# Two folded 512x512 weight matrices by quarter blocks, seven block products each, with quarter sums on Pool

## The chip, the cores and the metric

The kernel runs on one core of a Trainium2 chip. The metric is the device time of one execution in microseconds. The core has five engines with instruction streams of their own: PE (matmuls into PSUM), DVE (vector operations), ACT (scalar engine: activations and copies), POOL (GpSimd) and SP (which issues DMAs). [...]

## What is computed

Four layers follow each other on x of shape 8 x 512 x 32 x 32, in float32. The change touches layer 1, an attention with a residual, and stands in time beside layer 0. Cut to what matters:

```python
# layer 0: f, g, h are 1x1 convolutions to 64 channels; f and g get a batch norm and relu
z = einsum('bcn,bcm->bnm', f, g)
sigma = svd(z)[:, 0]                       # the largest singular value of each image
x = conv1x1(einsum('bnm,bcm->bcn', z / sigma, h), Wv) + x
# layer 1
h = group_norm(x)
q, k, v = wq @ h + bq, wk @ h + bk, wv @ h + bv
attn = softmax(einsum('bcn,bcm->bnm', q, k) * scale)
x = x + wp @ einsum('bnm,bcm->bcn', attn, v) + bp
# layers 2 and 3 follow
```

Since q'k is h'(wq'wk)h up to terms in the biases, and wp and wv stand next to each other, the kernel forms two 512x512 matrices once, on the chip: `wu` from q and k, `wo` from v and p. They are used for all eight images.

## The kernel before

The weights come with the contraction on the partitions. 512 channels are four chunks of 128 partitions, so a 512x512 matrix is a tile of 128 x 4 x 512. The program has three parts.

First, layer 0 streams through the eight images (L1225) while the weights are loaded. In the last image `natural` (L1191) turns q, k and v with PE transposes, evicted by ACT and DVE into `nat_q`, `nat_k`, `nat_v`. The batch-norm statistics of layer 0 then go through a serial piece: two small matmuls with `fold`, `rsqrt_eps` (L226 to L231: a power on Pool, L227, and small DVE operations), the relus on ACT (L1340), transposes of f and g (L1117), and gram matrices (L1312).

Second, `chain` squares a 128x128 matrix again and again to get sigma: two matmuls (L1008, L1009), an eviction on DVE and ACT, every second time also a trace (L1036, L1037, L1042) and a reciprocal and its powers (L1069 to L1072). Each step waits for the one ahead of it. To keep PE busy, a generator `filler` yields pieces of other work between the steps: the product that forms `wu`, further grams, the folded biases (L1290). The order of PE is written out by hand here: two filler pieces after one step, one after the next, and so on. After the chain, `entering` lets the first image into layer 1 (L403 to L436: residual, statistics, again a power on Pool), with the rest of the filler, at its end the product that forms `wo`. The orders of DVE, ACT and Pool are found by the scheduler.

A product is 16 matmuls of 128x128 by 128x512 in `product` (L1265), four for each 128 rows of the result, into `wide`, a PSUM tile of two banks, of which there are two. A `wide` is evicted whole by DVE or ACT (L1276, L1278).

Third, the main loop: for each image attention of layer 1, then layers 2 and 3. It begins with the first image: `normal` (eight L453 on DVE), `split_h` (four differences of quarters, L319 to L322), `make_u` (L380 with `wu`). The large products of the main loop already use the method that the change brings to the folding. `sums_of` and `differences_of` form sums and differences of quarters, and `seven` runs seven block products with their evictions: ACT copies at L331 and L342, DVE additions from PSUM at L337, and one addition on Pool at L352. `sums_u` (L1390) forms the sums of the quarters of the finished `wu`, four operations on DVE.

The functions that the diff touches, and what calls them:

Of the kernel before, what the change touches and what calls it, by code (L numbers as in the profile page):

```python
# [8 lines left out]
F32 = mybir.dt.float32  # L9
# [3 lines left out]
ALU = mybir.AluOpType  # L13
# [70 lines left out]
def kernel(  # L84
# [30 lines left out]
    def wide():  # L115
        return psum["wide"].tile([P, N], F32, tag="wide", name="wide")
# [4 lines left out]
    def bank():  # L121
        return psum["bank"].tile([P, HF], F32, tag="bank", name="bank")
# [17 lines left out]
    def half(i):  # L140
        return bass.ts(i, HF)
# [156 lines left out]

        return [t[:, rows[k], cols[m]] for m in range(2) for k in range(2)]

    def sums_of(a, more, queued=False):

        a11, a12, a21, a22 = a
        s1, s2, s4 = more
        tt = nc.vector.tensor_tensor
        first = tt(s1, a21, a22, ALU.add)
        if queued:
            tc.keep_in_program_order(first)
        tt(s2, s1, a11, ALU.subtract)  # L309
        tt(a21, a11, a21, ALU.subtract)  # L310
        tt(s4, a12, s2, ALU.subtract)
        return {"A11": a11, "A12": a12, "A22": a22, "S1": s1, "S2": s2, "S3": a21, "S4": s4}

    def differences_of(b, more):

        b11, b12, b21, b22 = b
        t1, t2, t4, t3 = (list(more) + [b12])[:4]
        tt = nc.vector.tensor_tensor
        tt(t1, b12, b11, ALU.subtract)  # L319
        tt(t2, b22, t1, ALU.subtract)  # L320
        tt(t3, b22, b12, ALU.subtract)
        tt(t4, b21, t2, ALU.subtract)  # L322
        return {"B11": b11, "B21": b21, "B22": b22, "T1": t1, "T2": t2, "T3": t3, "T4": t4}

    def seven(term, c11, c12, c21, c22, b1=None, b2=None, exp=None, then=None):
# [40 lines left out]
            then()  # L366
        yield

    def product_of(lt, rhs, view=None, parts=1):

        def term(ps, ka, kb, first, last):
            fresh = ps is None
            if fresh:
                ps = bank()
            w = HF // parts
            for q in range(parts):
                for k in range(2):
                    mm(  # L380
                        out=ps[:, q * w : (q + 1) * w],
                        lhsT=lt(ka, kb, q, k),
                        rhs=rhs(ka, kb, q, k),
                        start=first and q == 0 and k == 0,
                        stop=last and k == 1,
                        skip_group_check=True,
                    )
            return ps, ps if view is None else view(ps)

        return term  # L390
# [63 lines left out]
        return ht  # L454

    chunks = [slice(0, 2), slice(2, 4)]

    def split_h(env, ht):
        hs = env["big"].tile([P, 3, 2, HF], F32, tag="hs", name="hs")
# [725 lines left out]
    def natural(name, tag):  # L1185
        t = nat[name] = a1.tile([P, CC, C], F32, tag=tag, name="nat_" + name)
        for i in range(CC // 2):
            tp = wide().rearrange("p (o c j) -> p o c j", o=2, j=P)
            for k in range(2):
                for cc in range(CC):  # L1190
                    nc.tensor.transpose(  # L1191
                        tp[:, k, cc, :], sbw[name][:, cc, bass.ts(2 * i + k, P)], ident
                    )
            dst = t[:, 2 * i : 2 * i + 2, :].rearrange("p o (c j) -> p o c j", j=P)
            nc.scalar.copy(dst[:, 0], tp[:, 0])
            nc.vector.tensor_copy(dst[:, 1], tp[:, 1])
            yield
# [15 lines left out]
    for b in range(B):  # L1213
        xt = load_x(b) if b else first
        for name, src, pool in later.get(b, ()):
            load_w(name, src, shapes.get(name, [P, CC, C]), pool)
        if b == 4:
            load_rows()
        if b >= B - 2:
            resident[b] = xt  # L1220
        banks = [bank() for _ in w0]

        def products(i, cc):
            for h in range(NH):
                mm(  # L1225
                    out=banks[i][side(h), :],
                    lhsT=w0[i][:, cc, :],
                    rhs=xt[:, cc, half(h)],
                    start=cc == 0,
                    stop=cc == CC - 1,  # L1230
                )

        if b == 0:
            for cc in range(CC):
                for i in range(2):
                    products(i, cc)
        for i in range(3):
            if b == B - 1 and i == 2:
                for _ in natural("q", "w3"):
                    pass  # L1240
            if b or i == 2:
                for cc in range(CC):
                    products(i, cc)
            if i == 0:
                nc.scalar.copy(fs[b], banks[i])
                nc.vector.bn_stats(st[:, 0, b, :], fs[b])
            elif i == 1:
                nc.vector.tensor_copy(gs[b], banks[i])
                nc.vector.bn_stats(st[:, 1, b, :], gs[b])
                if last is not None:  # L1250
                    turn(last[0], last[1], ht_pair[last[0] // 2], 0)
        hraw = a2.tile([P, HF], F32, tag="hraw", name="hraw")
        nc.scalar.activation(hraw, banks[2], AF.Identity, bias=bhc)
        last = b, hraw
        if b == 3:
            total3 = sign_weights()
        if b == 5:
            scale_signs(total3)

    def product(lt, rhs, dst, vector):  # L1260
        for i in range(CC // 2):
            ps = wide()
            for k in range(2):
                for oc in range(CC):
                    mm(  # L1265
                        out=ps[:, half(k)],
                        lhsT=lt[:, oc, bass.ts(2 * i + k, P)],
                        rhs=rhs[:, oc, :],
                        start=oc == 0,
                        stop=oc == CC - 1,  # L1270
                    )
                    if k == 0 or oc < CC - 1:
                        yield
            to = dst[:, 2 * i : 2 * i + 2, :].rearrange("p o c -> p (o c)")
            if i % 2 and vector:
                nc.vector.tensor_copy(to, ps)  # L1276
            else:
                nc.scalar.copy(to, ps)  # L1278
            yield

    def biases():

# [23 lines left out]

    def gram(j, i, lt, rhs):
        ps = wide()  # L1310
        for t in range(NT):
            mm(  # L1312
                out=ps[:, 0:P],
                lhsT=lt[:, t, :],
                rhs=rhs[:, t, :],
                start=t == 0,
                stop=t == NT - 1,
            )
            if t == NT // 2 - 1:
                yield  # L1320
        nc.vector.tensor_tensor(gm[j][:, i, :], ps[:, 0:P], mask2, ALU.mult)
        yield
# [54 lines left out]
    def sums_u():  # L1377

        a11, a12, a21, a22 = quarters_of(wu, chunks, cols2)
        s1, s2, s4 = (su[:, i] for i in range(3))  # L1380
        weights["u"] = {
            "A11": a11, "A12": a12, "A22": a22, "S1": s1, "S2": s2, "S3": a21, "S4": s4
        }
        for args in (
            (s1, a21, a22, ALU.add),
            (s2, s1, a11, ALU.subtract),
            (a21, a11, a21, ALU.subtract),
            (s4, a12, s2, ALU.subtract),
        ):
            nc.vector.tensor_tensor(*args)  # L1390
            yield

    cols2 = [slice(0, C // 2), slice(C // 2, C)]

    def filler():

        yield from natural("v", "k")
        load_w("p", w_p, [P, CC, C], a1, tag="v")  # L1400
        yield from product(nat["q"], nat["k"], wu, True)
        yield from gram(jl, 2, ht_pair[jl], gtl)
        scale_z()
        yield
        between = biases()
        sums = sums_u()
        for j in rest:
            for _ in grams(j):
                next(sums, None)
                yield  # L1410
                if next(between, "end") != "end":
                    yield
        yield from product(nat["v"], sbw["p"], wo, False)

    todo = filler()
    for _ in range(5):
# [1 line left out]
    for ftl, gtl in turned_pair(jl):  # L1418
        pass
    for i, t in ((0, ftl), (1, gtl)):  # L1420
        for _ in gram(jl, i, t, t):
            pass

    relus = iter([(2 * j + k, i) for j in rest for i in range(2) for k in range(2)])
    with tc.manual_schedule(engines={mybir.EngineType.PE}):
        steps = entering(0)
        for k, _ in enumerate(chain(jl, True)):
            for _ in range(2 - k % 2 if k <= 2 * NSTEP else 4):
                next(todo, None)
            for args in (next(relus, None),):  # L1430
                if args:
                    relu(*args)
        for k in range(CC + 2):
            next(steps)
            for _ in range(3 if k < CC else 5):
                next(todo, None)
        for _ in todo:
            pass
# [193 lines left out]
```

## Time and profile before

The median of three runs is 1932.47 us (1932.23 to 1932.93). The profiled execution took 1932.7, its span is 1930.8 us, and the granted PE clock is 0.998.

| engine | busy us | instructions |
|---|---|---|
| PE | 1906.6 | 6230 |
| DVE | 1158.2 | 1875 |
| ACT | 507.7 | 807 |
| POOL | 229.7 | 178 |

| stretch (us from the start) | PE busy | DVE busy | POOL busy | what runs |
|---|---|---|---|---|
| 100 to 114 | 12.53 | 6.61 | 0.70 | statistics of layer 0, relus, first grams |
| 114 to 162 | 45.98 | 28.60 | 0.55 | squaring chain, with filler |
| 162 to 200.5 | 36.54 | 26.65 | 1.02 | first image into layer 1, product for `wo`, start of `make_u` |

A line of a timeline reads: start in us, duration in us, engine, line of the kernel, operation, output<-input, sizes, count; in brackets the idle time of the engine before it and what ended it. Neighbours of one kind are merged, with their number after x. A float32 matmul is two instructions for PE. In the view of busy time by stretch the columns are the stretch and its length, then busy time and instructions of PE, of the weight loads, DVE, ACT and POOL, the PE clock, the DMA share and GB/s.

### The profile page before, as it was taken

Reading aid. Unit: us, or ns where it says so; the run is one execution under the profiler, and the core shown is the slowest. Engines: PE = TensorE matmul, PEld = TensorE weight load, DVE = VectorE, ACT = ScalarE, POOL = GpSimd, SP = SyncE. Lnnn points to the kernel's source line nnn. Section 1 sums busy time; section 2 is a strip of 40 time slices with the busy share of each in tenths; the row PEclk is TensorE's granted clock in tenths of the full one; section 3 lists DMA queues with packets and bytes.
Section 4 is the critical chain, followed back from the end, with each engine's and each line's share of the span. In section 5 each row is a group of like instructions: output and inputs, shape, how many; then the busy total and the mean of one; then the engine's idle time right before and its main releaser. Section 6 shows DMA issues by size and latency. Waiting matters only on the chain.

```text
span 1930.8 us, 16673 instructions
## 1 busy us (share of the span) xinstructions
PE 1906.6 (99%) x6230; PEld 987.4 (51%) x6230; DVE 1158.2 (60%) x1875; ACT 507.7 (26%) x807; POOL 229.7 (12%) x178
## 2 busy tenths in 40 slices
PE   9999999999999999999999999999999999999997
PEld 4367456544655447454555446544645455544653
DVE  3256677448764687537754676348663775466647
ACT  2141222135222332025212331034202421143114
POOL 0000001200111001300121011201120011201121
PEclk9999999999999999999999999999999999999999
DMA  8420000002000120002000120002000200010001
GB/s 319 154 77 7 1 6 12 1 11 87 17 1 0 33 71 12 1 11 87 17 1 1 33 71 11 1 11 87 11 0 1 84 15 11 0 33 22 11 1 46
DMA packets 27784, 66.47 MB, mean 34 GB/s; under 512 B 4272, under 2 KB 5424, under 8 KB 27056
## 3 DMA queue, kind: packets, MB, share of 16 engines
q1 hardware_dynamic: 26768, 64.90, 10.0%
q8 instruction: 51, 0.84, 0.2%
q10 hardware_dynamic: 864, 0.43, 0.1%
q14 instruction: 37, 0.30, 0.1%
q0 software_dynamic: 64, 0.00, 0.0%
HBM read 38.51 MB, written 18.87 MB: 30 GB/s over the span
## 4 chain that ended last, share of the span: by engine, by line
PE 91%; DVE 7%; ACT 1%; issue 1%; DMA 0%; POOL 0%; DVEq 0%; ACTq 0%
PE bank L380 41%; PE bank L547 20%; PE bank L937 6%; PE bank L796 6%; PE bank L1225 4%; PE bank L648 3%; PE bank L403 2%; PE bank L665 2%; PE bank L1008 1%; PE wide L1265 1%; DVE both L739 1%; DVE both L709 1%; PE bank L1009 1%; PE wide L1312 1%; PE bank L688 1%; PE bank L817 1%
## 5 line engine op out<-in xcount | busy, mean ns | idle before, releaser
L547 PE MATMUL bank<-e,vt 128*128 128x512 f32 x768 | 334.0, 593 | 0.0
L547 PEld LDWEIGHTS bank<-e,vt 128*128 128x128 f32 x768 | 145.0, 190 | 175.4 <-issue 173.2
L380 PE MATMUL bank<-ut,h 128*128 128x512 f32 x384 | 181.3, 596 | 0.0
L337 DVE TENSOR_TENSOR e<-bank,e 128x512 f32<-128x512 f32 x128 | 87.6, 684 | 61.1 <-PE bank L380 60.3
L380 PE MATMUL bank<-us,hs 128*128 128x512 f32 x256 | 122.1, 599 | 1.3 <-DVE us L309 0.5
L380 PEld LDWEIGHTS bank<-ut,h 128*128 128x128 f32 x384 | 71.5, 190 | 85.8 <-issue 83.6
L937 PE MATMUL bank<-e,tpg 128*128 128x512 f32 x256 | 114.7, 595 | 0.0
L796 PE MATMUL bank<-tpg 128*128 128x512 f32 x256 | 114.6, 592 | 0.0
L803 ACT ACTIVATE e<-bank 128x512 f32<-128x512 f32 x128 | 76.5, 597 | 128.5 <-PE bank L796 128.5
L352 POOL TENSOR_TENSOR e<-e 128x512 f32<-128x512 f32 x32 | 44.1, 1378 | 419.5 <-ACT e L331 419.5
L380 PE MATMUL bank<-wo,h 128*128 128x256 f32 x384 | 91.8, 382 | 0.0
L808 DVE TENSOR_TENSOR esum<-esum,e 128x1024 f32<-128x1024 f32 x48 | 58.8, 1226 | 54.5 <-ACT e L803 54.5
L380 PE MATMUL bank<-h,wu 128*128 128x512 f32 x192 | 90.3, 593 | 0.7 <-ACT ut L342 0.7
L337 DVE TENSOR_TENSOR vt<-bank,vt 128x512 f32<-128x512 f32 x64 | 44.0, 688 | 70.5 <-PE bank L380 70.0
L937 PEld LDWEIGHTS bank<-e,tpg 128*128 128x128 f32 x256 | 48.1, 190 | 63.2 <-issue 63.1
L796 PEld LDWEIGHTS bank<-tpg 128*128 128x128 f32 x256 | 48.6, 190 | 60.8 <-issue 60.5
L352 POOL TENSOR_TENSOR ut<-ut 128x512 f32<-128x512 f32 x16 | 21.7, 1359 | 478.2 <-ACT ut L333 478.2
L380 PEld LDWEIGHTS bank<-wo,h 128*128 128x128 f32 x384 | 71.6, 190 | 13.5 <-ACT vt L331 4.1
L380 PEld LDWEIGHTS bank<-us,hs 128*128 128x128 f32 x256 | 46.7, 190 | 56.0 <-issue 46.4
L676 ACT ACTIVATE sg<-xt,rb 128x512 f16<-128x512 f32 x64 | 45.0, 718 | 103.7 <-DVE xt L667 100.2
L825 DVE RECIPROCAL rsum<-bank 128x512 f32<-128x512 f32 x15 | 50.3, 3356 | 28.6 <-PE bank L817 28.6
L1225 PE MATMUL bank<-xt,fg 128*64 128x512 f32 x256 | 59.7, 614 | 4.5 <-DMA fg<-in_w_fg 4.5
(325 smaller groups left out, 3090.1 us busy)
## 6 DMA issues: line engine op xcount, KB each, us to landing
xt<-in_x SPq DMA_DIRECT2D x55, 512.0 KB
out<-both SPq DMA_DIRECT2D x63, 256.0 KB
rfull<-rsum SPq DMA_DIRECT2D x60, 128.0 KB
f_dram<-f SPq DMA_DIRECT2D x8, 256.0 KB
fb<-f_dram SPq DMA_DIRECT2D x8, 256.0 KB
w<-in_w SPq DMA_DIRECT2D x1, 1024.0 KB
q<-in_w_q SPq DMA_DIRECT2D x1, 1024.0 KB
k<-in_w_k SPq DMA_DIRECT2D x1, 1024.0 KB
```

The source lines that it names most:

```text
L337: nc.vector.tensor_tensor(dst, ps, u, ALU.add)
L352: nc.gpsimd.tensor_tensor(c22, c22, c12, ALU.add)
L380: mm(out=ps[:, q * w : (q + 1) * w], lhsT=lt(ka, kb, q, k), rhs=rhs(ka, kb, q, k), start=first and q == 0 and k == 0, stop=last and k == 1 ...
L547: mm(out=ps, lhsT=a[:, t, bass.ts(r_, P)], rhs=e[t], start=first and t == 0, stop=last and t == NTH - 1, skip_group_check=True,)
L648: mm(out=ps[:, i, :], lhsT=xt[:, cc, bass.ts(4 * h + i, P)], rhs=sbw["tpg"][:, cc, 2 * P : 3 * P], start=cc == 0, stop=cc == CC - 1,)
L676: nc.scalar.activation(sg[:, cc, :], xt[:, cc, half(h)], AF.Sign, bias=rb3[:, cc : cc + 1])
L796: mm(out=ps, lhsT=pt[:, 0, bass.ts(t, P)], rhs=tt[:, 0, half(h)], start=True, stop=True,)
L803: nc.scalar.activation(e[:, half(h)], ps, AF.Exp, scale=float(P) ** -0.5)
L808: nc.vector.tensor_tensor(esum, esum, e, ALU.add)
L825: nc.vector.reciprocal(r, ps)
L937: mm(out=banks[h], lhsT=gt[:, t, :], rhs=es[t][:, half(h)], start=t == 0, stop=t == NT - 1,)
L1225: mm(out=banks[i][side(h), :], lhsT=w0[i][:, cc, :], rhs=xt[:, cc, half(h)], start=cc == 0, stop=cc == CC - 1,)
```

## The change

The two products are formed by 2x2 blocks of 256x256. Instead of eight block products there are seven (the form of Strassen and Winograd, as in the main loop), with four sums of the quarters of one factor (S1 to S4), four differences of the other (T1 to T4), and seven additions per block row in the evictions. Of the sums, those of q, v and p, and T3 and T4 of k, go to Pool; T1 and T2 of k to DVE. A term's result is 128x256 in half of a `wide`. The first two grams take `bank` instead of `wide` for their PSUM, and the number of filler pieces taken at the end changes. It is for less matmul work on PE: 7 block products of 8.

```diff
-    def sums_of(a, more, queued=False):
+    def sums_of(a, more, queued=False, eng=nc.vector):
...
-        tt = nc.vector.tensor_tensor
+        tt = eng.tensor_tensor
...
-    def differences_of(b, more):
+    def differences_of(b, more, engs=(nc.vector,) * 4):
...
+        for eng, (to, first, second) in zip(
+            engs, ((t1, b12, b11), (t2, b22, t1), (t3, b22, b12), (t4, b21, t2))
+        ):
+            op = eng.tensor_tensor(to, first, second, ALU.subtract)
+            if eng is nc.gpsimd:
+                tc.keep_in_program_order(op)
...
-    def product_of(lt, rhs, view=None, parts=1):
+    def product_of(lt, rhs, view=None, parts=1, source=bank, width=HF):
...
+                sums_q = sums_of(
+                    quarters_of(nat["q"], chunks, cols2),
+                    [so[:, i] for i in range(3)],
+                    eng=nc.gpsimd,
+                )
...
-    def product(lt, rhs, dst, vector):
-        for i in range(CC // 2):
-            ps = wide()
-            for k in range(2):
-                for oc in range(CC):
-                    mm(
...
-            if i % 2 and vector:
-                nc.vector.tensor_copy(to, ps)
-            else:
-                nc.scalar.copy(to, ps)
-            yield
+    def differ(rhs, to, engs):
+        b = [rhs[:, chunks[k], cols2[n]] for k in range(2) for n in range(2)]
+        return differences_of(b, to, engs)
+
+    def product(ab, dst):
...
+        for i in range(2):
+            term = product_of(
+                lambda ka, kb, q, k: a[ka][:, k, bass.ts(i, P)],
+                lambda ka, kb, q, k: b[kb][:, k, :],
+                source=lambda: next(source),
+                width=C // 2,
+            )
+            lo, hi = dst[:, i, :], dst[:, 2 + i, :]
+            yield from seven(term, lo[:, cols2[0]], lo[:, cols2[1]], hi[:, cols2[0]], hi[:, cols2[1]])
...
-    def gram(j, i, lt, rhs):
-        ps = wide()
+    def gram(j, i, lt, rhs, source=wide):
+        ps = source()
...
+        t3 = a1.tile([P, 2, C // 2], F32, tag="absw", name="t3")
+        engs = (nc.vector, nc.vector, nc.gpsimd, nc.gpsimd)
+        qk = sums_q, differ(nat["k"], [su[:, i] for i in range(3)] + [t3], engs)
...
-        yield from product(nat["q"], nat["k"], wu, True)
+        yield from product(qk, wu)
...
+                elif vp is None:
+                    vp = (
+                        sums_of(
+                            quarters_of(nat["v"], chunks, cols2),
+                            [so[:, i] for i in range(3)],
+                            eng=nc.gpsimd,
+                        ),
+                        differ(sbw["p"], [free[:, i] for i in range(3)], (nc.gpsimd,) * 4),
+                    )
-        yield from product(nat["v"], sbw["p"], wo, False)
+        yield from product(vp, wo)
...
-        for _ in gram(jl, i, t, t):
+        for _ in gram(jl, i, t, t, bank):
...
-            for _ in range(3 if k < CC else 5):
+            for _ in range(3 if k <= CC else 6):
```

## The prediction

> **What bounds it now.** I read the page first, then busy time by stage, then the timelines of the stretch that the change touches (100 to 200 us). The first two lines are from the page, the next three from the view of busy time by stretch.
>
> ```profile
> span 1930.8 us, 16673 instructions
> ...
> PE 1906.6 (99%) x6230; PEld 987.4 (51%) x6230; DVE 1158.2 (60%) x1875; ACT 507.7 (26%) x807; POOL 229.7 (12%) x178
> ...
> 100.00:114.00 14.00, 12.53 (x79) 8.88 (x77) 6.61 (x23) 10.06 (x16) 0.70 (x1) 1.00 0.54 189
> 114.00:162.00 48.00, 45.98 (x320) 38.00 (x321) 28.60 (x119) 15.26 (x35) 0.55 (x1) 1.00 0.06 23
> 162.00:200.50 38.50, 36.54 (x168) 21.35 (x168) 26.65 (x63) 6.31 (x10) 1.02 (x1) 1.00 0.03 8
> ```
>
> PE is busy nearly all the time, so less matmul work is worth its full length, unless PE then waits for something else. Between 100 and 200 us it idles only 5.5 of 100 us, and Pool does almost nothing (three instructions). But in this stretch PE is full because the products L1265 are filler between the steps of serial chains: statistics of layer 0, then the squaring chain (L1008, L1009, L1042), then the statistics of layer 1. Two timelines show these chains.
>
> ```profile
> 103.07 0.70 POOL L227 TENSOR_TENSOR r_r<-r_v,minus_half 128x2 f32<-128x2 f32 x1 [91.68 <-DVE r_v L226]
> 103.80 0.16 DVE L228 TENSOR_TENSOR r_e<-r_r 128x2 f32<-128x2 f32 x1 [0.20 <-POOL r_r L227]
> ...
> 105.70 1.52 ACT L1340 ACTIVATE f<-f,bi,r_r 128x512 f32<-128x512 f32 x2 [1.57 <-DVE bi L1370]
> ...
> 114.09 0.49 PE L1008 MATMUL bank<-gm 128*128 128x128 f32 x2 [0.38 <-DVE gm L1321]
> ```
>
> A tiny power on Pool releases six tiny DVE operations, these the relus, these the transposes and grams, these the squaring chain. Whatever delays DVE at 104 us delays 114.09.
>
> ```profile
> 189.20 7.11 PE L1265 MATMUL wide<-p,nat_v 128*128 128x512 f32 x16
> ...
> 192.18 3.74 DVE L453 TENSOR_SCALAR h<-xt,r_r,bi 128x512 f32<-128x512 f32 x8
> 195.83 1.22 DVE L319 TENSOR_TENSOR hs<-h 128x1024 f32<-128x1024 f32 x1
> ...
> 200.52 1.88 PE L380 MATMUL bank<-hs,su 128*128 128x512 f32 x4
> ```
>
> DVE normalises the first image while PE still runs the second product. By the chain of waits PE leaves that product at 196.31 and goes on into L380 with no wait for h.
>
> [...]
>
> ```profile
> 702.28 0.16 DVE L1070 TENSOR_TENSOR r<-r 128x1 f32<-128x1 f32 x1
> ...
> 710.28 1.26 POOL L352 TENSOR_TENSOR e<-e 128x512 f32<-128x512 f32 x1 [14.83 <-ACT e L331]
> ...
> 710.57 0.99 DVE L1070 TENSOR_TENSOR r<-r 128x1 f32<-128x1 f32 x1
> ```
>
> The same 128x1 product takes 0.16 us alone and ends with the Pool instruction otherwise (710.28 + 1.26 against 710.57 + 0.99). [...]
>
> **The change, part by part.**
>
> *Matmuls.* Before: 16 of 128x512 per product; a f32 matmul is two instructions in the trace, and the chain of waits gives 6.97 us for 16 of them, so 0.871 each, 13.9 per product. After: 2 x 7 x 2 = 28 of 128x256; no such product exists yet, but L380 bank<-wo,h has that shape, and 16 of its instructions run in 3.46 us, so 0.433 each, 12.1. Saved: 1.8 per product, **-3.6 us** for both. In the built order each of seven terms is one filler step of 0.87 us, as one 512-wide matmul was.
>
> *To the first chain matmul.* The DVE order now has T1 and T2 (0.68 each, as L1390) between the pieces of the mean and variance; about half a microsecond falls into waits that are there, so the power starts 0.85 later. Behind it Pool has T3 and T4, 1.27 us each (L352 alone 1.26). They are ready and start as the power ends, just when DVE wants its operations L228, L229 and so on, which read two SBUF tensors. T3 holds the first for up to 1.3 and T4 the next for about 1.0: +2.2. PE has S3*T3 queued ahead of the transposes, but it is done before the relus are. The first two grams write bank instead of wide, which removes the wait of 0.48 at 111.68. Sum **+2.5**. The four sums S of q start on Pool at 96 and end at about 101.2, before the power: nothing. The 128x256 evictions there sit in waits of ACT and DVE.
>
> *In the squaring chain* (114.09 to the last L1042 at 161.57, 47.5 us). The product gives 11 filler steps where it gave 13, so two more steps of grams and biases are drawn in: 1.8 us of PE work leaves and about as much enters. What changes is DVE. For each step it has an eviction wu<-wide,wu of about 0.42 [...], and ACT copies of wu stand between relus and the chain's copies. Walking the built order with these durations, PE waits about 0.8 more than before. [...]from the fourth term of the second row block Pool runs S1, c22, S2, S3, S4 of v and T1, T2 of p back to back, some 9 us. In it DVE has the copy rep, r2, r4, diag and two sums L1402. I count waits of 0.9 (rep), 1.0 (r4), 0.5 (r2 and diag), 1.0 and 0.8 (sums) = **4.2**; the bounds are 0 (each falls into slack) and 7 (all six wait 1.2). The fillers hide little, since the chain's evictions queue behind these on DVE. Sum +5.0.
>
> *After the chain.* 1.8 us of grams are already done, the second product is 1.8 shorter, and a wait for a bank at 171 us (0.8) shrinks by half: 34.7 us to the end of that product become 30.7: **-4.0**. Its S and T on Pool are ready long before.
>
> *Into layer 1.* The built DVE order puts four evictions wo<-wide,wo, the last of the last term, in front of the eight L453. So h starts 0.65 after PE has ended the product (latency, 0.42, a memset) where before it had started 4.1 earlier. PE's first matmul waits for two of the eight (0.94): +1.6. S2*T2 needs all eight and both 1.22 differences: 0.65 + 3.74 + 2.4 = 6.8 after the product's end; before it was 200.52 - 196.31 = 4.2. **+2.6**, and everything behind shifts; the order from there on is the same in both.
>
> Sum: 2.5 + 5.0 - 4.0 + 2.6 = **+6.1**, and 1932.5 + 6.1 = 1938.6; I say 1938.5.
>
> **Rivals.** *Waits hidden*: [...]Pool's run falls beside PSUM-source operations, which L618 shows unharmed (0.69 with Pool running). Then the start costs 0.7, the chain 0.8: 0.7 + 0.8 - 4.0 + 2.6 = +0.1, 1932.6, and with half of the collisions 1935. For it: Pool and DVE alternate in the trace. [...] *The saving arrives*: PE idles no more than now, because h isn't on the path or the start's delay is taken up: -3.6 and the gram's -0.5, 1928.4. For it: 99% PE. Against: the DVE order in front of L453. *Pool becomes the bound*: every DVE operation in its run waits and it stretches until terms wait too: +10, 1942.5. For it: at 325 us two Pool operations against a full DVE took 5.06 instead of 2.5. Against: the S and T have tens of us of slack.
>
> **Numbers.** Forecast 0.62, hidden 0.22, saving 0.07, Pool bound 0.09. Leaving out the saving and most of the Pool-bound case gives 1932 to 1942. Slower by over 0.2% is above 1936.3: most of the forecast, all of the last case: 0.68. Faster is below 1928.6: 0.07. The rest 0.25.
>
> **What would show it.** Right: L228 and its like lasting about 1 us at 105 to 108 us; the first chain matmul near 116.6; sums L1402 and r2, r4 of 1 us and more around 130; all L453 after the last L381 of the second product, and PE idle there; the stretch after 210 us the same but shifted. Wrong: tiny DVE operations at 0.16 throughout, or L453 running beside the product.

## The result and the profile after

The changed kernel takes 1944.56 us (median; 1944.19 to 1945.91), the kernel before 1932.57 beside it: the ratio is 1.0063, with a 95% interval of 1.0046 to 1.0081. It is 12.0 us slower. The forecast was 1938.5, slower by 6.

From the page after, and from its view of busy time by stretch (the columns as before: PE, weight loads, DVE, ACT, POOL, then the PE clock):

```profile
span 1944.0 us, 16826 instructions
...
PE 1907.5 (98%) x6278; PEld 997.1 (51%) x6278; DVE 1171.9 (60%) x1892; ACT 509.1 (26%) x816; POOL 249.6 (13%) x196
...
100.00:114.00 14.00, 10.99 (x73) 8.49 (x72) 9.84 (x25) 7.65 (x14) 4.65 (x5) 1.00 0.41 139
114.00:162.00 48.00, 43.59 (x310) 39.38 (x308) 29.67 (x105) 15.84 (x37) 9.78 (x9) 0.96 0.10 37
162.00:200.50 38.50, 33.45 (x215) 25.87 (x214) 26.17 (x75) 8.36 (x17) 4.24 (x4) 1.00 0.03 8
```

Three things are to be seen. PE is less busy in all three stretches: it does less work and waits for the rest. Pool went from 0.55 to 9.78 us in the squaring chain. And the clock of PE, 1.00 in every stretch before, is 0.96 in the chain.

For the ledger I took five moments from the timelines of PE: the start of the last convolution of layer 0 (`bank<-xt,h`), the first chain matmul, the last L1042 of the chain (L1044 after), the end of the product for `wo` (product 2 from here on), and the first S2\*T2 of layer 1 (`hs,su`). The first of them lies ahead of everything that the change touches, and yet it stands at 94.5 us before, at 94.9 after, and between 93.3 and 95.0 in the traces of the experiments, because their executions did not begin alike (the last section has what the traces show of it). So the times are counted from there, and not from the start of the span. The same five moments carry all experiments below (us):

| kernel | last convolution to first chain matmul | chain | chain to end of product 2 | from there to S2\*T2 | in all |
|---|---|---|---|---|---|
| before | 19.6 | 47.5 | 34.7 | 4.2 | 106.0 |
| after | 21.5 | 53.8 | 35.9 | 6.6 | 117.7 |
| own banks | 23.2 | 51.8 | 30.7 | 6.6 | 112.3 |
| memsets on Pool | 19.7 | 49.2 | 35.9 | 6.6 | 111.4 |
| own banks and memsets | 21.1 | 47.4 | 30.7 | 6.6 | 105.7 |
| own banks, ACT in place of the last additions | 23.0 | 51.8 | 30.7 | 4.2 | 109.7 |

(In the first stage of the own banks, and of the kernel with ACT, PE ran at half clock for 6.8 us and so lost 3.4; in that of the own banks and memsets it did for 3.4 us and lost 1.7.) From before to after the four stages are +1.9, +6.3, +1.1 and +2.4, together 11.7. Behind S2\*T2 the two traces run in parallel but for one place at 304 to 309 us, where the second chain loses another 1.05. That is 12.8 for the profiled execution, which was the slowest of the four; the medians lie 12.0 apart.

**The start**, as the timeline after shows it. Pool's T3 and T4 stand against two tiny operations that took 0.16 us each before:

```profile
105.08 1.26 POOL L321 TENSOR_TENSOR t<-nat_k 128x512 f32<-128x512 f32 x1
105.53 0.83 DVE L228 TENSOR_TENSOR r_e<-r_r 128x2 f32<-128x2 f32 x1
106.30 1.27 POOL L321 TENSOR_TENSOR su<-nat_k,su 128x512 f32<-128x512 f32 x1
106.39 1.20 DVE L229 TENSOR_TENSOR r_e<-r_e,r_v 128x2 f32<-128x2 f32 x1
```

L228 ends at 106.36, just after T3 (106.34), L229 at 107.59, just after T4 (107.57). From the start of the power L227 to the first relu it is now 4.28 us, where it was 2.63.

**The chain.** The timeline around 130 us shows the same with Pool's S and T of v and p, and what came of it on PE:

```profile
130.36 0.98 DVE L1072 TENSOR_TENSOR r<-r 128x1 f32<-128x1 f32 x1
131.28 1.26 POOL L310 TENSOR_TENSOR nat_v<-nat_v 128x512 f32<-128x512 f32 x1
131.37 1.19 DVE L1074 TENSOR_TENSOR r<-r 128x1 f32<-128x1 f32 x1
...
133.26 2.08 PE L381 MATMUL wide<-su,nat_q 128*128 128x256 f32 x4 [2.36 <-DVE wu L338]
...
137.16 1.75 DVE L1402 TENSOR_TENSOR su<-wu,su 128x512 f32<-128x512 f32 x1
```

L1072 and L1074 are r2 and r4, 0.16 each without Pool; the sum L1402 takes 0.68 without it. Behind r4 stand the chain's own copy L1032 and then the eviction L338, and PE's next term waits 2.36 us for that eviction. Its four matmul instructions then take 2.08 instead of 1.03, and the view by stretches of 1 us tells why: the PE clock, the third column from the end, falls to a half.

```profile
133.00:134.00 1.00, 0.74 (x2) 0.65 (x3) 1.00 (x3) 0.04 (x1) 0.77 (x1) 0.61 0.00 0
134.00:135.00 1.00, 1.00 (x4) 0.82 (x3) 1.00 (x3) 0.00 (x0) 0.00 (x0) 0.50 0.00 0
```

**Product 2.** The view of PE's waits between 100 and 215 us has two lines at its top that were not there before:

```profile
PE wide L381 <- DVE wo L338: 3.9, 4, 1.5
PE wide L381 <- DVE wu L338: 2.9, 2, 2.4
```

Waited in total, times, longest: 6.8 us for evictions of terms. What such a wait is made of shows in the timeline:

```profile
190.35 0.69 DVE L416 BATCH_NORM_STATS2 st<-xt 128x6 f32<-128x512 f32 x1
190.97 0.73 DVE L413 SCALAR_TENSOR_TENSOR xt<-bank,bvo,xt 128x512 f32<-128x512 f32 x1
191.62 0.41 DVE L338 TENSOR_TENSOR wo<-wide,wo 128x256 f32<-128x256 f32 x1
...
192.09 1.13 PE L381 MATMUL wide<-free,so 128*128 128x256 f32 x4 [1.49 <-DVE wo L338]
```

A term's result sits in one half of a `wide`; the next new term is to go into its other half. PE doesn't write that half until the first one is evicted, and the eviction stands on DVE behind the statistics of the first image. Of each row block, three of the seven evictions are copies on ACT and four are additions on DVE; the additions are not seven, as the text on the change has it. Product 2 has six such waits of PE, 3.9 us for additions on DVE and 0.9 for copies on ACT, and all six are for the term in the other half of the same tile. The 2.36 us in the chain are a wait of this kind too.

**Into layer 1** (timeline): h starts when the last addition of product 2 is done.

```profile
206.09 0.42 DVE L338 TENSOR_TENSOR wo<-wide,wo 128x256 f32<-128x256 f32 x1 [1.22 <-PE wide L381]
...
206.57 3.60 DVE L454 TENSOR_SCALAR h<-xt,r_r,bi 128x512 f32<-128x512 f32 x8
...
212.62 1.98 PE L381 MATMUL bank<-hs,su 128*128 128x512 f32 x4 [0.88 <-DVE hs L321]
```

### The profile page after: what moved, and what is told of

Read it like the earlier page. It is cut to its first block, busy times and chain, and to the rows that moved or that the text cites. A ratio compares the mean times of both kernels' runs of the same rounds, so it can differ in the third digit from the quotient of the medians.

```text
span 1944.0 us, 16826 instructions
## 1 busy us (share of the span) xinstructions
PE 1907.5 (98%) x6278; PEld 997.1 (51%) x6278; DVE 1171.9 (60%) x1892; ACT 509.1 (26%) x816; POOL 249.6 (13%) x196
## 4 chain that ended last, share of the span: by engine, by line
PE 89%; DVE 8%; ACT 1%; issue 1%; DMA 0%; POOL 0%; DVEq 0%; ACTq 0%
PE bank L381 40%; PE bank L549 20%; PE bank L939 6%; PE bank L798 6%; PE bank L1227 4%; PE bank L650 3%; PE bank L404 2%; PE bank L667 2%; PE bank L1010 1%; DVE both L741 1%; DVE both L711 1%; PE wide L381 1%; PE bank L1011 1%; PE bank L690 1%; PE wide L1324 1%
## 5 line engine op out<-in xcount | busy, mean ns | idle before, releaser
L338 DVE TENSOR_TENSOR e<-bank,e 128x512 f32<-128x512 f32 x128 | 87.6, 684 | 61.4 <-PE bank L381 60.3
L353 POOL TENSOR_TENSOR e<-e 128x512 f32<-128x512 f32 x32 | 44.1, 1379 | 419.5 <-ACT e L332 401.3
L338 DVE TENSOR_TENSOR vt<-bank,vt 128x512 f32<-128x512 f32 x64 | 44.0, 688 | 70.4 <-PE bank L381 70.0
L353 POOL TENSOR_TENSOR ut<-ut 128x512 f32<-128x512 f32 x16 | 21.8, 1360 | 477.2 <-ACT ut L334 477.2
```

The source lines that it names most:

```text
L338: nc.vector.tensor_tensor(dst, ps, u, ALU.add)
L353: nc.gpsimd.tensor_tensor(c22, c22, c12, ALU.add)
```

## The experiments

### One product at a time

Two kernels each keep one product in the old form (the old `product` beside the new one).

```diff
-        yield from product(vp, wo)
+        yield from product0(nat["v"], sbw["p"], wo, False)
```

> Only the first product (wu) by seven block products; the second as in the kernel before. If the start costs 1.9 us, the chain without Pool's run about 1, and one product saves 1.8 us of PE: about 1933.5. Rival, the evictions on DVE alone lengthen the chain by its 6 us, whatever Pool does: 1938.

Measured: 1933.15 (1932.67 to 1934.33) beside 1931.77 of the kernel before, ratio 1.0008 [0.9999, 1.0017], so +1.4.

```diff
-        yield from product(qk, wu)
+        yield from product0(nat["q"], nat["k"], wu, True)
```

> Only the second product (wo) by seven block products, its sums and differences on Pool; the first as in the kernel before. Tile waits of 4.8, the normalisation behind the last evictions 2.4, less 1.8 of PE: +5.4, and up to 2 more where Pool's eight operations meet the chain: 1938 to 1940. Rival, the second product gains as was forecast (-1.8, then +2.4 for the normalisation): 1933.

Measured: 1940.13 (1938.61 to 1940.71), ratio 1.0038 [1.0024, 1.0052], +8.4. With `wu` alone the first stage is 1.9 longer than before, as in the kernel after; the chain takes 49.2, the stage behind it 32.1, and the 4.2 after product 2 stay. With `wo` alone the chain takes 48.0, and the two stages behind it 4.2 more than before. Another 3.0 are lost ahead of the chain, without any T3 or T4 of k: Pool then runs the sums of v at 105 to 110 us, two of DVE's operations on the statistics take 1.26 and 1.11, and PE, which idles meanwhile, then loses 1.7 at half clock. So most of the loss hangs on product 2 and on its sums, which start as soon as they can.

### A bank for each term

```diff
-        def parts():
-            while True:
-                t = wide()
-                for h in range(2):
-                    yield t[:, h * HF : h * HF + C // 2]
...
-                source=lambda: next(source),
+                source=lambda: one()[:, 0 : C // 2],
```

`one` is a tile of one bank; there are four in place of two `wide`. The transposes of the weights and the grams take it too.

> As the changed kernel, but the two-bank tiles wide of this stage become single-bank tiles, so that no two block products (and no two halves of a transpose) share a tile; nothing else changes. Theory tile: in the changed kernel PE waits for the eviction of one term before it may start the next in the other half of the same wide (3.9 us on DVE wo and 0.9 on ACT wo in the second product, up to 2.9 on DVE wu in the first). Then the second product loses these 4.8 us and the chain another 1 to 2: about 1938. [...]

Measured: 1938.88 (1938.74 to 1939.05), ratio 1.0036 [1.0021, 1.0050], +7.1, against +12.0 of the change as it is. (The rival, that the tiles do not matter, stood for 1943.5 to 1944.5.) In the table, chain to end of product 2 falls from 35.9 to 30.7, and the chain from 53.8 to 51.8, where PE's clock now stays at 1.00. The matmuls, their order and the evictions' engines are the same, and twice as many tiles of half the size hold the same PSUM. In the timeline the term that waited 1.49 us starts without a wait, ahead of the eviction that it waited for:

```profile
187.82 1.03 PE L387 MATMUL one<-free,so 128*128 128x256 f32 x4
188.35 0.73 DVE L419 SCALAR_TENSOR_TENSOR xt<-bank,bvo,xt 128x512 f32<-128x512 f32 x1
...
189.00 0.41 DVE L344 TENSOR_TENSOR wo<-one,wo 128x256 f32<-128x256 f32 x1
```

So the wait was for the tile's other half. As tiles of their own the same halves hold nothing up: it is the program that waited for the tile as a whole. The gain would be larger but for the first stage, which is 1.8 longer than after the change: the relus are as late (13.7 us after the convolution, 13.8 after the change), but PE behind them runs at half clock, for 6.8 us.

### Pool without reading

```diff
-        tt = eng.tensor_tensor
+        if eng is nc.gpsimd:
+            tt = lambda to, x, y, op: tc.keep_in_program_order(eng.memset(to, 0.01))
+        else:
+            tt = eng.tensor_tensor
```

(and the same in `differences_of`; the sums on Pool are left out)

> As the changed kernel, but every sum and difference on Pool is a memset of the same tile, which reads no SBUF; the values of the products are therefore not those of the reference. [...]the tiny two-input operations of DVE are back at 0.16 us (L228 0.83 and L229 1.20 at 105 us, two of about 1 us at 130), the first chain matmul comes about 1.7 us earlier, PE no longer waits 2.4 us at 131 and its clock stays at full speed there (1.7 us more): 4 to 5 us less, about 1940. Rival tile alone: the waits on the evictions stay and the time changes by under 1 us, 1944.

Measured: 1938.28 (1937.64 to 1938.92), ratio 1.0034 [1.0021, 1.0046], +6.5. The first stage is 1.7 us shorter than after the change, as expected, and 0.2 longer than before it; the chain is 4.6 shorter. r2, r4 and the sums L1402 have 0.16 and 0.68 again, and the clock stays at 1.00. What is left: the 35.9 and the 6.6 of the last two stages, which Pool has nothing to do with. A memset takes 0.52 where a sum takes 1.27, so this run shortens Pool's work as well as taking away its reads. But the timeline shows two of the tiny operations inside a memset, and it doesn't hold them:

```profile
104.23 0.52 POOL L325 MEMSET su<- 128x512 f32 x1
104.25 0.15 DVE L228 TENSOR_TENSOR r_e<-r_r 128x2 f32<-128x2 f32 x1
104.43 0.16 DVE L229 TENSOR_TENSOR r_e<-r_e,r_v 128x2 f32<-128x2 f32 x1
```

So it is not only the length of Pool's work that holds DVE: beside its sums the same two took 0.83 and 1.20. That its reads make the difference is an estimate from these four times.

### Both

> Both edits that were measured apart, together: each term its own single-bank tile, and the Pool sums and differences replaced by memsets of 0.01 (the sums and differences of the quarters on Pool are left out). [...]first chain matmul at 113.4 and a chain of 49.2 as with the memsets alone, 30.7 from there to the end of product 2 as with the own tiles alone, S2*T2 6.6 later, near 199.8, which is 0.7 before its place in the kernel before; with the 1.0 that the second chain loses later, 1932.1, that is 0 to 0.5 above the kernel before. Rival: they are one cost seen twice [...], then together they give no more than the better of the two, 1938.

Measured: 1933.26 (1931.87 to 1934.15) beside 1932.11, ratio 1.0005 [0.9997, 1.0013], +1.2, where 0 to 0.5 was expected. That S2\*T2 stands at 199.7 us of the span, as expected to 0.1, is luck: the first chain matmul came at 115.1 instead of 113.4, since PE lost 1.7 at half clock ahead of it, and the chain is 1.8 shorter than expected. The stages are what shows that the two costs are separate: product 2 has the 30.7 of the own banks, and the chain is shorter than with either edit alone. It takes 47.4, no more than before the change; so of its extra 6.3 us Pool's sums make 4.6 (53.8 to 49.2) and the shared tile 1.8 (49.2 to 47.4). Taken in the other order they are 4.4 and 2.0.

### The additions in front of the normalisation

On top of the own banks; ACT copies the terms of the second row block of product 2, where DVE added (the additions are left out).

```diff
         def plus(ps, bias, u, dst):
-            if bias is None:
+            if act:
+                nc.scalar.copy(dst, ps)
+            elif bias is None:
```

> Own single-bank tiles; in the second row block of product 2 the additions on DVE are left out, and ACT copies each term instead (the additions of that block are left out). Theory: layer 1 starts late because the eight normalisation operations stand behind the last additions of product 2 on DVE. Without them h starts with the statistics and runs beside product 2, and PE loses its 2.4 us of waits: 1936.5 against 1938.9 of the own tiles alone. Rival: the statistics themselves come late now, since the filler is shorter and DVE busier, and h waits for them: then less than 1 us is won, 1938 to 1939.

Measured: 1935.87 (1934.74 to 1937.14), ratio 1.0019 [1.0012, 1.0027], +3.8 where the own banks had +7.1. The timeline:

```profile
196.38 4.15 DVE L462 TENSOR_SCALAR h<-xt,r_r,bi 128x512 f32<-128x512 f32 x8
...
203.04 1.92 PE L389 MATMUL bank<-hs,su 128*128 128x512 f32 x4
```

h starts 2.5 us ahead of the end of product 2 (198.84), S2\*T2 follows that end by 4.2, the figure of before, and PE doesn't wait for it. Only these evictions moved, so they were what held h. The other 0.9 of the gain lies in the second chain, whose extra 1.05 is nearly gone in this trace (0.05). There one addition of Pool (L353 of the kernel after) meets one sum of DVE (L570). Before the change, and here, Pool's takes 2.05 and DVE's 0.69; after it, Pool's takes 1.26 and DVE's 1.42. With the memsets the order is that of the kernel after and the 1.05 is lost again, so the sums of the quarters are not its cause: which of the two comes first changed when everything behind was shifted.

### The same sums at another time

Three kernels remain, and in them nothing is left out. The first adds to the own banks a tiny operation on Pool ahead of T3 and T4 of k, and two ahead of the sums of v and the differences of p; each reads a result that lands late, so that the sums can't start sooner. And A12\*B21 goes third in the first row block, so that PE has a term that needs no sum.

```diff
+        behind_of(t3[:, 0, 0:1], bi0[:, 0:1])
         qk = sums_q, differ(...)
...
-                elif vp is None:
+                elif vp is None and j == rest[1] and k == 3:
+                    behind_of(so[:, 0, 0, 0:1], gm[j][:, 0, 0:1])
+                    behind_of(free[:, 0, 0, 0:1], gm[j][:, 0, 0:1])
```

> The whole computation. Own single-bank tiles; T3 and T4 of k on Pool wait for the last operation of the layer 0 statistics, and the term A12*B21 takes the third place in the first row block, so that PE does not wait for T3; the sums of v and the differences of p on Pool wait for a gram that lands near the end of the squaring chain[...]. [...]same work on Pool at another time costs nothing, so it comes out as with the memsets: first chain matmul at 113.4, chain 49.2, 30.7, 6.6, in all 1932.1 (0 to 0.5 above the kernel before). Rival: the cost of Pool's sums is not their place but their length, Pool's run collides with the statistics of the first image instead: 1935 to 1937.

Measured: 1935.36 (1932.51 to 1936.47), ratio 1.0015 [1.0008, 1.0021], +3.2. Half right. The chain takes 47.5, where own banks and memsets had 47.4, with Pool's full work: its place was what cost there. The first stage takes 20.4, although PE lost 1.7 in it at half clock; the late sums and the moved term both help there, and this run doesn't tell them apart. But the gram landed at 160.9, earlier than I had thought, and Pool's run fell on the last piece of the chain:

```profile
161.37 1.23 DVE L1051 TENSOR_TENSOR diag<-gm 128x128 f32<-128x128 f32 x1
...
162.94 0.88 DVE L1096 TENSOR_TENSOR ln<-ln,quarters 128x11 f32<-128x11 f32 x1
...
165.07 2.47 DVE L1102 TENSOR_SCALAR gm<-gm,rsig 64x128 f32<-64x128 f32 x2
```

Before, these took 0.29, 0.17 and 0.59. The stage behind the chain is 34.2 instead of 30.7, with 1.7 of it from PE at half clock. The runs fall into two groups: the seven with a granted clock of 0.998 or more took 1932.5 to 1934.0, the fourteen with less 1934.7 to 1936.5.

The next one keeps this, puts the term that ACT evicts (A12\*B21) last in the second row block, and gives four of the eight normalisation operations to ACT.

```diff
+        if third == "last":
+            yield
+            fifth()
...
-                if cc % 2 and not alone:
+                if cc % 2:
                     nc.scalar.activation(hs, xs, AF.Identity, bias=b1, scale=s1)
```

> The whole computation: as the late sums, and at the end of product 2 the term A12*B21, which ACT evicts, goes last, and four of the eight normalisation operations of the first image go to ACT. By the same theory h is complete about 1.2 us earlier after the end of product 2 (5.4 instead of 6.6): 1931, 0.5 to 1.3 below the kernel before. Rival: ACT's four operations end later than DVE's would have, or the gain is lost to a wait in the main loop: 1932 to 1933.

Measured: 1933.01 (1932.06 to 1935.60), ratio 1.0009 [1.0001, 1.0018], +0.9. The mechanism holds (5.6 from the end of product 2 to S2\*T2, instead of 6.6, where 5.4 was expected). The total missed: Pool's run is still at 162 to 172, and the stage behind the chain takes 32.8. The median hides two groups here too, seven runs of 1932.1 to 1933.0 and six of 1934.9 to 1935.6; those six all have a granted clock of 0.997, as have two of the seven.

The last one moves that run behind a gram of the last pair, in the order S1, S2, T1, T2, S3, T3, S4, T4, and takes S1\*T1 ahead of S3\*T3 in the first row block, so that PE has one more term ahead of the transposes.

```diff
-                elif vp is None and j == rest[1] and k == 3:
+                elif vp is None and j == rest[2] and k == 3:
...
-    for _ in range(5):
+    for _ in range(6):
         next(todo)
```

> The whole computation: as the kernel with A12*B21 last, and three more moves. The sums of v and differences of p on Pool wait for a gram of the last pair, some 12 us later, past the end of the squaring chain, where the trace shows them holding four operations of its last piece for 0.4 to 2 us each; their order on Pool is S1, S2, T1, T2, S3, T3, S4, T4, as the terms need them; and S1*T1 goes before S3*T3 in the first row block, so that one more term fills the gap of 1.7 us of PE ahead of the transposes. Theory: every extra wait of the changed kernel has its own operation, and moved away it is gone: about 1.5 us at the end of the chain and 0.9 at the start, 1930.5 to 1931, that is 1 to 1.5 below the kernel before. Rival: the 3.6 us of matmuls saved do not come out because the chain and the statistics set the pace, and filler taken out of them is idle time: 1932 to 1933, like the kernel before.

Measured: 1929.98 (1929.01 to 1931.58) beside 1931.91 of the kernel before, ratio 0.9990 [0.9981, 0.9998]: 1.9 us faster than before, and some 14 faster than the change as it was. From its page and its timeline:

```profile
PE 1902.9 (99%) x6278; PEld 995.7 (52%) x6278; DVE 1162.3 (60%) x1888; ACT 511.5 (27%) x820; POOL 250.5 (13%) x199
```

```profile
161.96 0.29 DVE L1059 TENSOR_TENSOR diag<-gm 128x128 f32<-128x128 f32 x1
...
164.70 0.58 DVE L1110 TENSOR_SCALAR gm<-gm,rsig 64x128 f32<-64x128 f32 x2
```

PE is busy 3.7 us less than before (1906.6), the 3.6 that the forecast worked out for the matmuls. The end of the chain has its old durations again. The stages are 19.6, 47.8, 30.9 and 5.6, together 103.9: 2.1 ahead of the kernel before, and the whole run behind it keeps that distance. Of the saving, the 1.4 by which the last stage is longer than before is what is still missing.

## Why the forecast was right and wrong

- **Matmuls, -3.6.** Right: 3.7 less busy PE in the last kernel. In the kernel after the page doesn't show it (1907.5 against 1906.6), since 1.7 us of half clock count as busy there, and a term of four instructions counts 1.13 behind a wait and 1.03 behind another term.
- **To the first chain matmul, +2.5.** Right: +1.9, by the waits named (L228, L229). Its parts hold too: the power comes 1.0 later (0.85 was said), the two held operations add 1.7 (2.2 was said), and from the relus to the first chain matmul it is 0.7 less (0.5 was said). With the memsets the two take 0.15 and 0.16, and +0.2 is left.
- **Squaring chain, +5.0.** Right in kind, small in size: +6.3. What Pool's sums cost DVE and the chain was put at 4.2 and makes 4.6; but in the profiled run 1.7 of that is PE at half clock after a wait of 2.36 us, of which the forecast knew nothing, and the direct waits are less. The evictions were put at 0.8 and make 1.8, because of the shared tile: with own banks and memsets the chain is no longer than before. The length of one on DVE, 0.42, was right: 128x256 takes 0.41 to 0.43 in the trace after.
- **After the chain, -4.0.** This is the step that failed: +1.1. The term "30.7 us to the end of product 2" is the right number for a kernel in which each term has its own bank, which measures 30.7; in the kernel as it was the stage takes 35.9, and 4.8 of the 5.2 us on top stand in its trace as waits for the other half of a `wide`. The forecast saw the words "a term's result is 128x256 in half of a `wide`" and even counted a wait for a bank (0.8 us, to shrink by half), but took halves for separate buffers. The diff held the warning: `parts()` gives out two halves of one tile, one after the other, with an eviction between.
- **Into layer 1, +2.6.** Right: +2.4 (4.2 to 6.6), and the ACT evictions take just that away.
- **The rest unchanged.** Nearly: one meeting of Pool and DVE in the second chain went the other way round, +1.05.

The sum of the steps was 6.1 and should have been 11.7 at S2\*T2; the failed step alone makes 5.1 of the difference. Every sign that was named for being right came true, from L228 to the idle PE ahead of h; none of them looked at product 2. Of the rivals, "waits hidden" would have been off by more. "Pool becomes the bound" had a time nearer to the result, but not its reason: Pool's terms were ready in time in product 2.

## What to carry to other kernels

Ask of every small result in a large PSUM tile which unit the waits are kept by: two results in one tile made a write of the second wait for the eviction of the first here, and that eviction stood behind others on DVE (35.9 us for the stage, 30.7 with own tiles). Count what shifting work to an idle engine does to the smallest operations of a serial chain beside it (0.16 us became 0.83 and 1.20 here), and if it hurts, tie the moved work to a late result rather than leave it to start as soon as it can. When a saving is 0.2% of the time, as the 3.6 us are here, one queue in front of the wrong operation takes back most of it (2.4 into layer 1); look at the order behind the last eviction. And count stages from a moment ahead of the change: the executions here differ by up to 1.7 us before anything of it has run (93.3 to 95.0).

## What was not expected of the hardware

PE's clock falls in steps of equal cost. The traces show it at a half after gaps of PE of 2.36 us (after), 2.21 (own banks, and with ACT), 2.12 (`wo` only), 1.89 (own banks and memsets) and 1.70 (late sums). Each time PE ran at half clock for 3.41 us, and for 6.82 after the gaps of 2.21, so the loss, one minus the clock summed over the stretch, was 1.7 us, or twice that. With another gap of 1.70 (A12\*B21 last) and one of 1.76 (own banks) the clock stayed at 1.00, and between 90 and 138 us it fell after no gap of 1.5 or less alone. The late sums have one more slow place, behind a gap of 0.94: from 168.57 us four instructions of L417 take 2.08 us, where four of the same line take 1.13 from 173.96 on.

In two traces the moments at which the clock changes can be compared: they are whole multiples of 3.4133 us apart. In the kernel after, the record of the clock begins with full speed at 10.34 us, it falls at 133.22, which is 36 of them later, and rises again at 136.63. In the kernel before, the record begins at 9.96 and the clock falls at 1924.84, behind the last matmul, which is 561 of them later. In the 3.41 us that end at the drop PE was busy for 1.10 us in the kernel after, and for 1.13 (own banks), 1.44 (with ACT), 1.30 (`wo` only), 1.33 (own banks and memsets) and 1.67 (late sums). The gap of 1.76 that cost nothing lies from 133.66 to 135.42, across 134.06, which is eight multiples behind the drop of that trace at 106.75; the 3.41 us ahead of 134.06, which also hold a part of a gap of 1.32, have 1.69 us of work. So where a gap lies may count as much as its length; that is an estimate from these few gaps. The slow place at 168 us, with one gap of 0.94 ahead of it, doesn't fit, and I have no account of it.

So the wait of 2.36 us in the chain cost 4.1 in all, and another of 1.76 no more than itself. A part of the scatter between runs of one kernel can be such drops, an estimate from the 1.7 us of one; the two groups of the late sums, some 2 us apart and with different granted clocks, fit it. The last convolution of layer 0 starts between 93.3 and 95.0 us in the eleven traces. From before to after it is 0.36 later, and the first matmul, which waits for a DMA, is 0.35 later already (4.53 and 4.88 us); where the rest of the 1.7 comes from was not shown. Up to about the moment at which the record of the clock begins, PE has half its later pace in both traces: two matmul instructions start every 0.85 us ahead of it, every 0.43 behind it.

A second point: in the stretches above, a tiny operation of DVE that meets Pool's run ends with one operation of Pool, and one of 0.16 us takes 0.6 to 1.26, at most about the length of one Pool operation of 1.27. It isn't always DVE that waits: in the trace before, at 325 us, a sum of Pool takes 2.86 while three sums of DVE run beside it at 0.68 each; behind it Pool's next takes 2.25, and one of DVE 1.68 instead of 0.68. An operation that is one line of the timeline with x2, as L1102 (2.47), pays twice: it took 0.59 before.
